# Twelve-bit gated projection: halves of the output product behind the first and second block of the next quarter, value halves added up in PSUM

## The chip, the core and the metric

The kernel runs on one core of a Trainium2 chip. The core has a matrix engine (PE, with a separate lane PEld for the weight loads), a vector engine (DVE), a scalar engine (ACT), a general engine (POOL) and a queue that issues transfers (SP). Each takes its instructions in the order of its own queue; an instruction starts when the results it needs are there. PE writes into PSUM, which has eight banks of 128 x 512 numbers here; DVE and ACT read and write PSUM and SBUF, POOL only SBUF. The metric is the device time of one execution in microseconds (us); the median of three runs before is 2509.24 us (2509.1 to 2509.75).

## The reference

The inputs are 1024 rows of 512 numbers, a graph, and 16 blocks of conditions. A graph layer is followed by four equal layers of cross attention and a gated feed-forward part, and a second graph layer. The change touches the feed-forward part alone:

```python
for i in range(L):                              # L = 4
    a = _attn(_ln(h, ...), cond, Wq[i], Wk[i], Wv[i], Wo[i])
    h = h + a
    u = _ln(h, ln3_w[i], ln3_b[i]) @ geglu_w[i] + geglu_b[i]    # 512 -> 4096
    val, gate = jnp.split(u, 2, axis=-1)
    f = val * jax.nn.gelu(gate, approximate=False)              # 1024 x 2048
    h = h + f @ ffo_w[i] + ffo_b[i]                             # 2048 -> 512
```

## The kernel before

All large products are made by a scheme that needs seven block products where eight are usual (two by two blocks; the sums of blocks that it needs are made by POOL and DVE). The 2048 columns of the feed-forward part are taken in four **quarters** r of 512, and each quarter in four **blocks** c of 128 columns. One block yields `f` for its 128 columns and all 1024 rows: two tiles of 128 x 512, here f0 and f1 (`a11`/`a12` and `a21`/`a22` of the output product). When the four blocks of a quarter are there, `ffn_out` (L1309) multiplies them with the quarter's output weights and adds to `h`. It does so in two **halves** s = 0, 1, each seven products of eight PE instructions. In a half the products run in the order 0, 6, 4, 5, 1, 3, 2. Products 0 and 6 read only tiles of blocks 0 and 1. Products 4, 5 and 2 read the sums `fs` (s1, s2, s4), which need blocks 2 and 3. Products 1 and 3 add to the banks of 0 and 6, so they wait until DVE has read those: `kept` (L1329) and `hall` (L1325).

Quarter 0 is made with plain 32-bit products (class `Quad`, with the banks ga, gb, gc, gd). Beside it ACT and DVE split the normalised rows into high and low parts (`begin_right` L1084 makes gr, `finish_right` L1093 makes gl), because quarters 1 to 3 are made with "twelve-bit" products: both factors split into a high part and a low part, three matmuls for one (class `Chunk`, L1113). A Chunk's weights are loaded by four transfers (`__init__`, tiles gxa and gxb), summed by POOL (`sums`, L1139, the last sum into gy), and split by `split` (L1101: ACT makes the high part gha or ghb, DVE the low part gla or glb, POOL the third factor gsa or gsb); the part with the suffix a serves products 0, 5, 6, 4, the part with b products 1 and 3. Product 2 stays a 32-bit product, made from gy (L1215). In the tables all banks of a Chunk are called g.

`Chunk.steps` (L1184) is a generator: between its yields the main loop (L1801) runs parts of the block before. Before, one turn of the loop for block n gives PE this order: the first parts of products 0 and 5 of n; then, of block n-1, product 2 into bank `d` (L1215, behind the DVE addition `add(g1, d, u3)` of L1209, shown as L1190, that has to read d first) and the end of product 1; the end of 0 and the first part of 6; the end of 3 of n-1; the end of 5; then the first parts of 4, 1 and 3 with the ends of 6 and 4 between. DVE has in a turn, in this order: the value v1 (L1218) and f1 = v1 x g1 (L1220) of n-1, the addition for u2 of n, f0 of n-1 (L1226), the sums of f of n-1 (`sums_of_f`, L1289: one subtraction for blocks 0 and 1, which POOL makes, L1294; three for blocks 2 and 3, on DVE, L1296 to L1298), u3, glb of n+1, the two additions onto scaled banks (L1173) with g1 between them, and gla of n+2 (L1104).

The order of nearly all of this is fixed: `pin` (L1099) puts an instruction behind the one traced before it on its engine. Instructions without `pin` are ordered by the scheduler of the language: the earliest in the program among those whose inputs it takes to be there, so that work from further down fills a wait. `ffn_out` is pinned for quarters 1 and 2, and not for quarters 0 and 3. For quarters 1 and 2 both halves stand behind the turn of block 0 of the next quarter (L1827).

Buffers: 36 slots of 128 x 1024 (`slots`), ten tiles of 128 x 512 (`work`, t512), six accumulators (`accs`), and two single tiles with the tags row and last (`rows`).

## Time and profile before

| | |
|---|---|
| median of the runs | 2509.24 us |
| time of the profiled execution | 2509.91 us |
| its span, first to last instruction | 2508.1 us |
| mean granted PE clock | 0.99 |
| ACT busy | 840.8 us (34%) |
| POOL busy | 1052.3 us (42%) |

The profile is of one execution. A row of waits names who waited, for which instruction, the sum, how often, and the longest. A row of the timeline has the start, the duration, engine, line, operation and tiles, and in brackets the idle time ahead of it and what ended that. A row by stage has, behind the bounds and the length, the busy time of PE, PEld, DVE, ACT and POOL with instruction counts, then the granted PE clock as a share of full speed, and the share of the transfer engines. A group row has count, busy time, mean duration in ns, and idle time ahead.

### The profile page before, as it was taken

Reading aid. Unit: us, or ns where it says so; the run is one execution under the profiler, and the core shown is the slowest. Engines: PE = TensorE matmul, PEld = TensorE weight load, DVE = VectorE, ACT = ScalarE, POOL = GpSimd, SP = SyncE. Lnnn points to the kernel's source line nnn. Section 1 sums busy time; section 2 is a strip of 40 time slices with the busy share of each in tenths; the row PEclk is TensorE's granted clock in tenths of the full one; section 3 lists DMA queues with packets and bytes.
Section 4 is the critical chain, followed back from the end, with each engine's and each line's share of the span. In section 5 each row is a group of like instructions: output and inputs, shape, how many; then the busy total and the mean of one; then the engine's idle time right before and its main releaser. Section 6 shows DMA issues by size and latency. Waiting matters only on the chain. (4 is left out here: it accounts for less than half of the span.)

```text
span 2508.1 us, 35093 instructions
## 1 busy us (share of the span) xinstructions
PE 2418.3 (96%) x13032; PEld 1887.7 (75%) x13032; DVE 1740.1 (69%) x3224; ACT 840.8 (34%) x1784; POOL 1052.3 (42%) x1083
## 2 busy tenths in 40 slices
PE   8999999998999999999999999999999999999999
PEld 5778886676787887567787888477777888567677
DVE  9666567877676557786686556786795556787764
ACT  7323334333223334342313334432223333432320
POOL 0433444366553223274563224254474322435641
PEclk9999999999999999999999999999999999999999
DMA  5422220111312210011222121011132031011140
GB/s 176 130 74 97 97 85 22 47 50 35 113 39 76 93 64 22 19 58 47 64 92 72 72 76 35 13 55 43 42 130 68 14 122 51 5 47 51 34 143 35
DMA packets 118066, 163.56 MB, mean 65 GB/s; under 512 B 9256, under 2 KB 66928, under 8 KB 117888
## 3 DMA queue, kind: packets, MB, share of 16 engines
q1 hardware_dynamic: 115792, 155.81, 19.1%
q0 software_dynamic: 1376, 4.30, 0.5%
q8 instruction: 107, 1.75, 0.3%
q10 hardware_dynamic: 720, 1.11, 0.1%
q14 instruction: 71, 0.58, 0.1%
HBM read 138.12 MB, written 23.07 MB: 64 GB/s over the span
## 5 line engine op out<-in xcount | busy, mean ns | idle before, releaser
L1105 POOL TENSOR_TENSOR gsa<-gha,gla 128x1024 fp32r<-128x1024 f32 x48 | 115.9, 2415 | 175.3 <-DVE gla L1104 170.5
L1169 ACT ACTIVATE g<-g 128x512 f32<-128x512 f32 x192 | 108.0, 574 | 238.1 <-PE g L1155 236.5
L799 ACT ACTIVATE pr<-sc,nmax 128x256 f32<-128x256 f32 x256 | 118.2, 471 | 91.9 <-DVE nmax L794 91.4
L1182 ACT ACTIVATE g<-g,gcols 128x512 f32<-128x512 f32 x96 | 67.5, 703 | 223.6 <-DVE g L1190 214.3
L300 PE MATMUL fa<-wff,fT 128*128 128x256 f32 x512 | 125.6, 386 | 14.2 <-DVE kept L1329 14.2
L1215 PE MATMUL g<-ln3T,gy 128*128 128x512 f32 x192 | 103.3, 665 | 37.2 <-DVE g L1190 37.2
L997 POOL TENSOR_TENSOR kr<-ct,ct 128x256 f32<-128x256 f32 x48 | 36.9, 768 | 211.8 <-DVE pr L804 207.2
L300 PEld LDWEIGHTS fa<-wff,fT 128*128 128x128 f32 x512 | 98.0, 193 | 34.6 <-DVE kept L1329 17.4
L300 PE MATMUL pa_v<-wv,ct 128*128 128x256 f32 x512 | 124.0, 385 | 0.0
L1155 PE MATMUL g<-gr,gsa 128*128 128x512 f32 x384 | 121.4, 398 | 0.9
L1155 PE MATMUL g<-gr,gha 128*128 128x512 f32 x384 | 122.0, 399 | 0.0
L1294 POOL TENSOR_TENSOR fT<-fT,fT 128x512 f32<-128x512 f32 x24 | 30.9, 1288 | 217.1 <-DVE fT L1226 217.1
L300 PE MATMUL pc_v<-wv,ct 128*128 128x256 f32 x512 | 121.0, 379 | 0.0
L300 PE MATMUL pd_v<-wvs,ct 128*128 128x256 f32 x512 | 121.0, 379 | 0.0
L1155 PE MATMUL g<-gl,gla 128*128 128x512 f32 x384 | 119.0, 391 | 0.0
L794 DVE TENSOR_REDUCE nmax<-sc 128x2 f32<-128x512 f32 x128 | 83.7, 678 | 41.2 <-PE sc L787 41.2
L1104 DVE SCALAR_TENSOR_TENSOR gla<-gha,gxa 128x1024 fp32r<-128x1024 f32 x48 | 76.5, 1594 | 51.3 <-ACT gha L1103 51.3
L300 PEld LDWEIGHTS pa_v<-wv,ct 128*128 128x128 f32 x512 | 94.9, 190 | 22.5 <-issue 9.2
L300 PEld LDWEIGHTS pd_v<-wvs,ct 128*128 128x128 f32 x512 | 97.3, 190 | 13.2
L300 PEld LDWEIGHTS pc_v<-wv,ct 128*128 128x128 f32 x512 | 97.0, 190 | 13.0
L1215 PEld LDWEIGHTS g<-ln3T,gy 128*128 128x128 f32 x192 | 37.4, 205 | 75.3 <-DVE g L1190 46.9
L804 DVE TENSOR_SCALAR pr<-pr,inv 128x256 f32<-128x256 f32 x256 | 90.4, 395 | 2.9
(518 smaller groups left out, 6474.5 us busy)
## 6 DMA issues: line engine op xcount, KB each, us to landing
ct<-cond_dram SPq DMA_DIRECT2D x72, 512.0 KB, 5.3
wff<-in_L_gnn_ffo_w_dram SPq DMA_DIRECT2D x32, 512.0 KB, 4.1
cond_dram<-ct SPq DMA_DIRECT2D x24, 512.0 KB, 3.0
gxa<-in_L_gnn_geglu_w_dram SPq DMA_DIRECT2D x96, 128.0 KB, 2.2
gxb<-in_L_gnn_geglu_w_dram SPq DMA_DIRECT2D x96, 128.0 KB, 2.2
cond<-in_L_gnn_cond_dram SPq DMA_DIRECT2D x32, 256.0 KB, 4.7
ct<-cond_dram SPq DMA_DIRECT2D x24, 256.0 KB, 5.6
wk<-in_L_gnn_Wk_dram SPq DMA_DIRECT2D x8, 512.0 KB, 4.3
```

The source lines that it names most:

```text
L300: each(nc.tensor.matmul(at, left[:, k, l0:l1], right[:, k, r0:r1], start=start and n == 0 and k == 0, stop=n == len(cols_of) - 1 and k == ...
L794: nc.vector.tensor_reduce(nmax, ps3, AX.X, OP.max, negate=True)
L799: nc.scalar.activation(pr3[:, a, :], ps3[:, a, :], AF.Exp, bias=nmax[:, a:a + 1], accum_out=tot[:, a:a + 1])
L804: scores.last = nc.vector.tensor_scalar(pr3[:, a, :], pr3[:, a, :], inv[:, a:a + 1], None, OP.mult)
L997: t.tensor_tensor(to, of, less, OP.subtract)
L1104: pin(nc.vector.scalar_tensor_tensor(l.bitcast(F32R), h, -1.0 / TINY, x, OP.mult, OP.add))
L1105: pin(nc.gpsimd.tensor_tensor(s.bitcast(F32R), h, l, OP.subtract))
L1155: pin(nc.tensor.matmul(to, self.part(i, which)[:, k, :], self.rights[i][which].bitcast(F32R)[:, k, :], start=start and k == 0, stop=stop a ...
L1169: pin(nc.scalar.mul(to, to, 1.0 + TINY))
L1182: pin(nc.scalar.activation(to, of, AF.Gelu, bias=gcols[:, cg:cg + 1]))
L1215: pin(nc.tensor.matmul(d, self.last[:, k, :], self.rights[2][:, k, :], start=False, stop=k == 1, skip_group_check=True))
L1294: each(t.tensor_tensor(a21, a11, a21, OP.subtract))
```

## The change

It has these parts:

- Within a turn the end of product 1 of block n-1 comes first, and product 2 of n-1 (into `d`) comes behind the end of product 3, so behind 22 instead of 12 twelve-bit PE instructions after the end of product 4.
- v1 and f1 are replaced: DVE adds u2 to d in PSUM (`add(d, d, u2)`), and f1 = (d + bias) x g1 is read from PSUM. f0 comes before them.
- All sums of f are made by DVE; they stand behind the turn, after the split of the low part, which itself moves from between u3 and the scaled banks to the end of the turn.
- The split of the next weights' high part and the load (`split_next`) move from the end of the turn for n+2 to the place behind the first two products, for n+1 (in the turns of blocks 1 to 3 of quarter 1 and block 3 of later ones, and of block 0 of quarters 2 and 3); for blocks 0 and 1 of quarters 2 and 3 one such split stands ahead of a half.
- The two halves of `ffn_out` of quarters 1 and 2 stand behind blocks 0 and 1 of the next quarter, one each. `ffn_out` of quarter 0 is pinned. The load of the next output weights follows the second half.
- The low parts gl for products 0 and 1 are made during quarter 0's third block, 5 and 6 ahead of the first half, 4 and 3 between the halves.
- `add_bias` runs for all eight row blocks at once ahead of quarter 0's end, where the last two were added at the layer's end.
- Buffers: `kept` is two t512 instead of a slot, gy takes the single tiles row and last, the tiles of f are taken block by block, and v1's accumulator is gone.

```diff
--- before.py
+++ after.py
...
@@ -1113,14 +1113,13 @@
     class Chunk:
 
 
...
         def __init__(self, l, r, c):
             self.n, self.c = f"{l}_{r}_{c}", c
             self.cv = l * 2 * DFF // P + r * KC + c
             self.x = [flat(slot(f"gxa_{self.n}")), t512(f"gxb_{self.n}")]
             if c % 2 == 0:
-                Chunk.room = t512(f"gy_{self.n}")
+                tag = ("row", "last")[c // 2]
+                Chunk.room = rows.tile([P, D], F32, tag=tag, name=f"gy_{self.n}")
             self.last = columns_of(Chunk.room)[:, c % 2]
             for k, n in enumerate((2, 1)):
                 for j in range(2):
@@ -1181,7 +1180,7 @@
             cg = self.cv + DFF // P
             pin(nc.scalar.activation(to, of, AF.Gelu, bias=gcols[:, cg:cg + 1]))
 
-        def steps(self, aside):
+        def steps(self, sum_next, split_low):
 
 
             n, bias = self.n, gcols[:, self.cv:self.cv + 1]
@@ -1199,31 +1198,29 @@
             yield
             add(u2, self.end(5), s1)
             yield
-            aside[0]()
+            sum_next()
             self.scale(4)
             add(u3, self.end(6), u2)
-            aside[1]()
             self.scale_onto(1, s1)
             g1 = acc_tile(f"g1_{n}")
             d = self.end(4)
             add(g1, d, u3)
             self.gate(g1, g1)
             self.scale_onto(3, u3)
-            aside[2]()
+            split_low()
             yield
-            for k in range(2):
-                pin(nc.tensor.matmul(d, self.last[:, k, :], self.rights[2][:, k, :], start=False,
-                                     stop=k == 1, skip_group_check=True))
-            v1 = acc_tile(f"gv1_{n}")
-            pin(nc.vector.scalar_tensor_tensor(v1, d, bias, u2, OP.add, OP.add))
-            f0, f1 = (self.fT[i][self.c // 2][:, self.c % 2, :] for i in range(2))
-            pin(nc.vector.tensor_tensor(f1, v1, g1, OP.mult))
             a = self.end(1)
             yield
             g0 = acc_tile(f"g0_{n}")
             self.gate(g0, self.end(3))
+            for k in range(2):
+                pin(nc.tensor.matmul(d, self.last[:, k, :], self.rights[2][:, k, :], start=False,
+                                     stop=k == 1, skip_group_check=True))
+            f0, f1 = self.f.of(self.c)
+            pin(nc.vector.scalar_tensor_tensor(f0, a, bias, g0, OP.add, OP.mult))
+            add(d, d, u2)
             yield
-            pin(nc.vector.scalar_tensor_tensor(f0, a, bias, g0, OP.add, OP.mult))
+            pin(nc.vector.scalar_tensor_tensor(f1, d, bias, g1, OP.add, OP.mult))
 
     class KeyPair(InStep):
 
@@ -1279,47 +1276,61 @@
         return {i: inner_right(nc.gpsimd, *(x[i][:, k, :] for k in range(2) for x in of), quarters(room))
                 for i, room in zip(INNER[0] + INNER[1], rooms)}
 
-    def f_slots(l, r):
-        return ([slots_of(2, f"fT_{l}_{r}_{i}") for i in range(2)], slots_of(3, f"fs_{l}_{r}"))
-
...
-    def sums_of_f(fT, s, c, t=nc.vector, each=lambda ins: ins):
-        k = c % 2
-        a11, a12, a21, a22 = (fT[i][j][:, k, :] for i in range(2) for j in range(2))
-        s1, s2, s4 = (x[:, k, :] for x in s)
-        if c < 2:
-            each(t.tensor_tensor(a21, a11, a21, OP.subtract))
-        else:
+    class Gated:
+
+
+        def __init__(self, l, r):
+            self.n, self.tiles, self.s = f"{l}_{r}", [], None
+
+        def of(self, c):
+            if c == len(self.tiles):
+                self.tiles.append(slot(f"fT_{self.n}_{c}"))
+            return [self.tiles[c][:, i, :] for i in range(2)]
+
+        def sums(self, c, t=nc.vector, each=lambda ins: ins):
+            if c < 2:
+                a11, a21 = self.of(c)
+                each(t.tensor_tensor(a21, a11, a21, OP.subtract))
+                return
+            if c == 2:
+                self.s = slots_of(3, f"fs_{self.n}")
+            (a11, a21), (a12, a22) = self.of(c - 2), self.of(c)
+            s1, s2, s4 = (x[:, c % 2, :] for x in self.s)
             each(t.tensor_tensor(s2, a22, a21, OP.subtract))
             each(t.tensor_tensor(s1, s2, a11, OP.add))
-            sums_of_f.last = each(t.tensor_tensor(s4, a12, s2, OP.subtract))
+            Gated.last = each(t.tensor_tensor(s4, a12, s2, OP.subtract))
+
+        def left(self):
+            blocks = [[self.of(2 * j + k)[i] for k in range(2)] for i in range(2) for j in range(2)]
+            return order7(blocks, *([x[:, k, :] for k in range(2)] for x in self.s))
+
...
     def ffn_out(l, r, s, left, right, kept, each=lambda ins: ins):
...
         n = f"{l}_{r}_{s}"
-        u = kept[:, s, :]
+        u = kept[s]
         a, b, c, d = (bank(f"{x}_{n}") for x in ("fa", "fb", "fc", "fd"))
         h11, h12, h21, h22 = (hall[:, 4 * i + 2 * s:4 * i + 2 * s + 2, j * M:(j + 1) * M]
                               for i in range(2) for j in range(2))
 
         def product(i, to, start):
-            multiply(to, left[i], right[i],
-                     [((2 * s + q) * P, (2 * s + q + 1) * P, 0, M) for q in range(2)], start,
-                     each)
+            for q in range(2):
+                for k in range(2):
+                    each(nc.tensor.matmul(to[:, q * M:(q + 1) * M],
+                                          left[i][k][:, (2 * s + q) * P:(2 * s + q + 1) * P],
+                                          right[i][:, k, :], start=start and q == 0 and k == 0,
+                                          stop=q == 1 and k == 1, skip_group_check=True))
 
         def add(to, of):
             each(nc.vector.tensor_tensor(to, halves_of(of), to, OP.add))
...
     def load_projections(l):
...
-        wv_summed = weight_sums.last
         next_cond(l, 0)
         wq, wo, ffb = load_rest(l)
-        with waiting_for(sums_of_f.last, mybir.EngineType.Pool):
-            with tc.issue_after(wv_summed.ins):
-                for nb in range(NB - 2, NB):
-                    summed = add_bias(nb)
-            with tc.issue_after(summed.ins):
-                wq = weight_sums(wq, f"wqs_{l}")
+        with waiting_for(Gated.last, mybir.EngineType.Pool):
+            wq = weight_sums(wq, f"wqs_{l}")
         return wk, wv, (wq, weight_sums.spare), wo, ffb, spare
 
     def load_last():
...
@@ -1736,7 +1742,7 @@
         ln3_turn(g, (1, 1))
         summed = ln3_sums(nc.vector, g)
         with tc.issue_after(summed.ins):
-            for nb in range(NB - 2):
+            for nb in range(NB):
                 add_bias(nb)
         quads[2].second()
         quads[3].second()
@@ -1744,20 +1750,27 @@
 
         last = l == L - 1
         lnT = None
-        kept = slot(f"kept_{l}")
+        kept = [t512(f"kept_{l}_{i}") for i in range(2)]
         raw_out = load_out(l, 0)
         more = [slot(f"gr_{l}_{i}") for i in range(2 * len(SPLIT) - 2)]
         wide = four_wide(f"gr_{l}")
         more.extend(wide[:, 2 * i:2 * i + 2, :] for i in range(2))
         begun = {i: (right[i], *more[2 * n:2 * n + 2]) for n, i in enumerate(SPLIT)}
+        Chunk.rights = {2: right[2]}
+
+        def finish_rights(*of):
+            for i in of:
+                Chunk.rights[i] = finish_right(f"gl_{l}_{i}", *begun[i])
 
         def parts_beside(c):
             with tc.issue_after(quads[c].last.ins):
                 for i in SPLIT[2 * c:2 * c + 2]:
                     begin_right(f"gt_{l}_{i}", *begun[i])
+                if c == 2:
+                    finish_rights(0, 1)
 
         wff = out_weights(nc.gpsimd, l, 0, raw_out)
-        geglu(quads, fT, fS, parts_beside)
+        geglu(quads, f, parts_beside)
         chunks = [(r, c) for r in range(1, R) for c in range(KC)]
         ready = []
 
@@ -1765,88 +1778,69 @@
             if chunks:
                 ready.append(Chunk(l, *chunks.pop(0)))
 
-        def prepare(n, *what):
+        def sum_chunk(n):
             if n < len(ready):
-                for do in what:
-                    if do is None:
-                        ready[n].sums()
-                    else:
-                        ready[n].split(do)
+                ready[n].sums()
+
+        def split(n, low):
+            if n < len(ready):
+                ready[n].split(low)
 
         load()
-        prepare(0, None)
-
-        def finish_rights(*of):
-            for i in of:
-                Chunk.rights[i] = finish_right(f"gl_{l}_{i}", *begun[i])
-
-        Chunk.rights = {2: right[2]}
-        finish_rights(0, 5)
-        ffn_out(l, 0, 0, left_of_f(fT, fS), wff, kept)
-        prepare(0, False, True)
-        finish_rights(6, 4)
+        sum_chunk(0)
+        finish_rights(5, 6)
+        ffn_out(l, 0, 0, f.left(), wff, kept, pin)
+        split(0, False)
+        split(0, True)
         load()
-        prepare(1, None)
-        ffn_out(l, 0, 1, left_of_f(fT, fS), wff, kept)
-        finish_rights(1, 3)
-        prepare(1, False)
+        sum_chunk(1)
+        finish_rights(4, 3)
+        ffn_out(l, 0, 1, f.left(), wff, kept, pin)
+        split(1, False)
         load()
         raw_out = load_out(l, 1)
 
-        def finish_chunk(flow, c):
-            next(flow, None)
-            sums_of_f(fT, fS, c, *((nc.gpsimd, pin) if c < 2 else (nc.vector, pin)))
+        def split_next(n):
+            split(n, False)
+            load()
 
         before = None
         for r in range(1, R):
             for c in range(KC):
                 chunk = ready.pop(0)
-
-                def sum_next():
-                    prepare(1, None)
-
-                def split_low():
-                    prepare(0, True)
-
-                def split_next():
-                    prepare(1, False)
-                    load()
-
-                flow = chunk.steps([sum_next, split_low, split_next])
+                flow = chunk.steps(lambda: sum_chunk(1), lambda: split(0, True))
+                chunk.f = f if c else Gated(l, r)
                 next(flow)
+                if c > 2 or r == 1 and c or r > 1 and c == 0:
+                    split_next(0)
+                for _ in range(3):
+                    if before:
+                        next(before, None)
+                    next(flow)
                 if before:
-                    next(before)
-                next(flow)
-                if before:
-                    next(before)
-                next(flow)
-                if before:
-                    finish_chunk(before, (c - 1) % KC)
-                next(flow)
+                    f.sums((c - 1) % KC, nc.vector, pin)
                 before = flow
                 if c == 0:
-                    if r > 1:
-                        for s in range(2):
-                            ffn_out(l, r - 1, s, left_of_f(fT, fS), wff, kept, pin)
+                    kept_f, f = f, chunk.f
+                if r > 1 and c < 2:
+                    split_next(1)
+                    ffn_out(l, r - 1, c, kept_f.left(), wff, kept, pin)
+                    if c == 1:
                         raw_out = load_out(l, r)
-                    fT, fS = f_slots(l, r)
-                elif c == (KC - 1 if r + 1 < R else KC - 2):
+                if c == (KC - 1 if r + 1 < R else KC - 2):
                     wff = out_weights(nc.gpsimd, l, r, raw_out)
-                chunk.fT = fT
-        for _ in range(2):
-            next(before)
-        finish_chunk(before, KC - 1)
-        fT = left_of_f(fT, fS)
+        for _ in range(3):
+            next(before, None)
+        f.sums(KC - 1, nc.vector, pin)
+        fT = f.left()
         if last:
             w_out, base, again, dinv_row = load_last()
-            with waiting_for(sums_of_f.last, mybir.EngineType.Pool):
-                for nb in range(NB - 2, NB):
-                    add_bias(nb)
+            with waiting_for(Gated.last, mybir.EngineType.Pool):
                 w_out = out_weights(nc.gpsimd, L, 0, w_out)
             ffn_out(l, R - 1, 0, fT, wff, kept)
         else:
             lnT = [slots_of(2, f"ln2T_{l + 1}_{i}") for i in range(2)]
-            projections = load_projections(l + 1, add_bias)
+            projections = load_projections(l + 1)
             ffn_out(l, R - 1, 0, fT, wff, kept)
             ready_first(l + 1, [0, 1, 4, 5])
             ffn_out(l, R - 1, 1, fT, wff, kept)
```

23 lines of the change are left out of this document (10 added, 13 removed).

## The prediction

> **What bounds the kernel now.** I read the page first. PE is the bound: it is busy nearly all of the span, so what can be won is PE's waiting.
>
> ```profile
> PE 2418.3 (96%) x13032; PEld 1887.7 (75%) x13032; DVE 1740.1 (69%) x3224; ACT 840.8 (34%) x1784; POOL 1052.3 (42%) x1083
> ```
>
> Then the waits of the weight loads, which show better than the modelled matmuls where PE stands still:
>
> ```profile
> PEld g L1215 <- DVE g L1190: 46.9, 23, 3.5
> ...
> PEld fa L300 <- DVE kept L1329: 17.4, 8, 3.7
> ...
> PEld fc L300 <- DVE hall L1325: 11.9, 4, 3.0
> ```
>
> All three are waits on DVE in the feed-forward part: product 2 waits for g1, a half for `kept`, quarter 0's second half for `hall`. The timeline of weight loads gives the pace: product 2 of the first and of the last block of each layer, and between them, in layer 0, one wait and two products of a half.
>
> ```profile
> 497.59 0.41 PEld L1215 LDWEIGHTS g<-ln3T,gy 128*128 128x128 f32 x2
> ...
> 532.67 0.50 PEld L1215 LDWEIGHTS g<-ln3T,gy 128*128 128x128 f32 x2 [3.52 <-DVE g L1190]
> ...
> 545.36 1.70 PEld L300 LDWEIGHTS fc<-wff,fT 128*128 128x128 f32 x8
> 547.09 1.70 PEld L300 LDWEIGHTS fd<-wffs,fs 128*128 128x128 f32 x8
> ...
> 677.80 0.30 PEld L1215 LDWEIGHTS g<-ln3T,gy 128*128 128x128 f32 x2 [1.90 <-DVE g L1190]
> ...
> 1081.44 0.41 PEld L1215 LDWEIGHTS g<-ln3T,gy 128*128 128x128 f32 x2
> ...
> 1260.85 0.30 PEld L1215 LDWEIGHTS g<-ln3T,gy 128*128 128x128 f32 x2 [1.86 <-DVE g L1190]
> ...
> 1664.50 0.41 PEld L1215 LDWEIGHTS g<-ln3T,gy 128*128 128x128 f32 x2
> ...
> 1844.68 0.30 PEld L1215 LDWEIGHTS g<-ln3T,gy 128*128 128x128 f32 x2 [1.87 <-DVE g L1190]
> ...
> 2248.34 0.41 PEld L1215 LDWEIGHTS g<-ln3T,gy 128*128 128x128 f32 x2
> ...
> 2424.86 0.41 PEld L1215 LDWEIGHTS g<-ln3T,gy 128*128 128x128 f32 x2
> ```
>
> And three stages of layer 0, each beginning where product 2 of a block begins:
>
> ```profile
> core 0: us, PE busy (x) PEld busy (x) DVE busy (x) ACT busy (x) POOL busy (x), PEclk, DMA share, GB/s
> 497.59:507.58 9.99, 9.99 (x41) 7.51 (x40) 9.04 (x10) 4.73 (x9) 6.79 (x6) 1.00 0.13 37
> 518.98:532.67 13.69, 10.49 (x40) 7.36 (x40) 12.21 (x14) 5.62 (x10) 10.40 (x10) 0.97 0.16 44
> 532.67:543.60 10.93, 10.92 (x31) 7.42 (x32) 7.02 (x8) 5.49 (x9) 7.87 (x6) 0.72 0.00 0
> ```
>
> From one product 2 to the next is one turn. The first stage is a turn of 9.99 in which PE never stands, the second one of 13.69 with the wait of 3.52. Where DVE has 9.04 of work PE does not wait; where it has 12.21, PE does. Behind the long wait the granted clock is 0.72 for 10.93, some 3 lost: a long wait is paid twice.
>
> A half is seven products at 547.09 - 545.36 = 1.73, so 12.1. Undisturbed, the eleven turns and four halves between a layer's first and last row take 11 x 9.99 + 4 x 12.1 = 158.3. They took 180.2, 179.4, 180.2 and 176.5: 21.9 + 21.1 + 21.9 + 18.2 = **83.1 us** too long. That is what can be won in quarters 1 to 3.
>
> **DVE's durations**, group means of layer 0's stretch from 480 to 705, with ACT's high part:
>
> ```profile
> L1220 DVE TENSOR_TENSOR fT<-gv,g 128x512 f32<-128x512 f32 x12 | 21.5, 1792 | 0.6
> L1104 DVE SCALAR_TENSOR_TENSOR gla<-gha,gxa 128x1024 fp32r<-128x1024 f32 x11 | 18.4, 1672 | 13.0 <-ACT gha L1103 13.0
> L1104 DVE SCALAR_TENSOR_TENSOR glb<-ghb,gxb 128x512 fp32r<-128x512 f32 x11 | 12.3, 1116 | 0.0
> ...
> L1218 DVE SCALAR_TENSOR_TENSOR gv<-g,gcols,gu 128x512 f32<-128x512 f32 x12 | 8.9, 744 | 9.0 <-PE g L1215 9.0
> ...
> L1226 DVE SCALAR_TENSOR_TENSOR fT<-g,gcols,g 128x512 f32<-128x512 f32 x12 | 8.9, 738 | 0.0
> L1297 DVE TENSOR_TENSOR fs<-fs,fT 128x512 f32<-128x512 f32 x6 | 8.3, 1392 | 0.2
> L1173 DVE SCALAR_TENSOR_TENSOR g<-g,gs 128x512 f32<-128x512 f32 x12 | 8.2, 685 | 0.0
> ...
> L1298 DVE TENSOR_TENSOR fs<-fT,fs 128x512 f32<-128x512 f32 x6 | 7.3, 1212 | 0.0
> L1296 DVE TENSOR_TENSOR fs<-fT,fT 128x512 f32<-128x512 f32 x6 | 6.1, 1013 | 0.0
> ```
> ```profile
> L1103 ACT ACTIVATE gha<-gxa 128x1024 fp32r<-128x1024 f32 x11 | 11.6, 1051 | 19.1 <-POOL gxa L1139 18.9
> ```
>
> Single rows of the timeline: f1 twice and a short gla on DVE, then POOL's two products of a split.
>
> ```profile
> 523.63 2.33 DVE L1220 TENSOR_TENSOR fT<-gv,g 128x512 f32<-128x512 f32 x1
> ...
> 534.36 1.23 DVE L1104 SCALAR_TENSOR_TENSOR gla<-gha,gxa 128x1024 fp32r<-128x1024 f32 x1 [1.13 <-ACT gha L1103]
> ...
> 647.76 0.69 DVE L1220 TENSOR_TENSOR fT<-gv,g 128x512 f32<-128x512 f32 x1
> ```
> ```profile
> 520.59 1.27 POOL L1105 TENSOR_TENSOR gsb<-ghb,glb 128x512 fp32r<-128x512 f32 x1
> 523.02 2.40 POOL L1105 TENSOR_TENSOR gsa<-gha,gla 128x1024 fp32r<-128x1024 f32 x1 [1.16 <-DVE gla L1104]
> ```
>
> f1 takes 0.69 alone and 2.33 while POOL makes gsa. Instructions that read a bank (L1173, L1218, L1226) keep to 0.69 to 0.74 in the mean, those on two SBUF tiles (f1, gla, glb, the sums) do not.
>
> **The change part by part.**
>
> *Value in PSUM.* v1 and f1 (0.744 + 1.792) become an addition into a bank (taken as L1173, 0.685, which also writes one; no row shows the very form) and an f1 with the form of f0 (0.738): 1.1 less on DVE a turn. A turn's eight instructions on banks are 6 x 0.685 + 2 x 0.738 = 5.6; with gla and glb (2.8) that is 8.4.
>
> *Sums of f.* Blocks 0 and 1: one subtraction comes from POOL to DVE, 0.69 free to 1.39 held: 9.1 to 9.8 a turn, under 9.99. Blocks 2 and 3: three, 1.0 + 1.4 + 1.2 = 3.6 held, 2.1 free: 10.5 to 12.0, over 9.99. Both of these now fall into the turn of block 0 of the next quarter. With the half behind it PE has 22.1 there, DVE 8.4 + 3.6 + 3.6 + 1.7 (a second gla) + 6 x 0.685 = 21.4.
>
> *Product 2 later, the end of product 1 earlier.* Product 2 is reached ten twelve-bit instructions later; a turn of 9.99 has 36 of them and product 2, which I put at one 1.73, so 8.26 / 36 = 0.23 each, 2.3 together. But the end of product 1 now stands where product 2 stood and waits for its scaled bank, which DVE makes one instruction (0.69) before g1. So the move alone wins only 0.69 of each wait; DVE's lighter turn has to win the rest. In the turns with 9.1 to 9.8 it does.
>
> *Split later.* Behind the first two products (8 x 0.23 = 1.8) come the high part (1.05), gla (1.7) and gsa (2.4): gsa ends some 7 into a turn and is needed behind ten instructions of the next, at 9.99 + 2.3 = 12.3. Some 5 are spare, and I cost it at nothing. Loads and POOL's weight sums move with it in SP's and POOL's queues; POOL loses the subtraction on which it stood waiting.
>
> *A half behind block 0, one behind block 1.* The second has DVE nearly free: no cost. In the first, product 4 needs s1 of block 3. Since the last turn's end DVE then has glb, three sums, gla, eight on banks, glb and two sums: 1.1 + 3.6 + 1.7 + 5.6 + 1.1 + 2.4 = 15.5 held, 0.7 + 2.1 + 1.2 + 5.6 + 0.7 + 1.4 = 11.7 free. PE gets there after 9.99 + 2 x 1.73 - 0.7 = 12.7. The wait is 0 to 2.8, with the clock's 3 up to 5.8. POOL has output weights to sum there, so I take 2.4, near the held end: two a layer, **+19** (0 to 46).
>
> *Quarter 0, pinned.* Its weight loads and one DVE row:
>
> ```profile
> 457.69 0.19 PEld L300 LDWEIGHTS fa<-wff,fT 128*128 128x128 f32 x1 [0.24 <-issue]
> ...
> 459.20 0.41 PEld L300 LDWEIGHTS gc<-ln3S,wgate 128*128 128x128 f32 x2
> ...
> 485.00 1.59 PEld L300 LDWEIGHTS fc<-wffs,fT 128*128 128x128 f32 x8 [2.97 <-DVE hall L1325]
> ...
> 488.35 0.41 PEld L1155 LDWEIGHTS g<-gr,gha 128*128 128x128 f32 x2
> ```
> ```profile
> 469.67 0.68 DVE L1297 TENSOR_TENSOR fs<-fs,fT 128x512 f32<-128x512 f32 x1
> ```
>
> Before, a half's product (fa) filled in ahead of block 3's own (gc) while DVE was late. Pinned, it cannot: products 0 and 6 follow block 3, product 4 waits for s1 (469.67 + 0.68 = 470.35), and from there twelve products remain, 20.8. Quarter 1 begins at 491.1 instead of 488.35: +2.8, the 2.97 being gone. The low parts for products 0 and 1 (1.2 each, as gla) now stand ahead of block 3's work on DVE, s1 up to 2.4 later; or one low part and an addition leave its way, 1.9 earlier. So 0.9 to 5.2, with the clock to 8.2; I take 3.5, close to the first figure: four layers, **+14** (4 to 33).
>
> *Layer's end.* Three sums (3.6) now stand ahead of block 3's f0, product 2 behind it is ready sooner. **+4** (-5 to +6, a sum or so a layer either way). `add_bias` and the buffers: the waits of PE above name neither, so nothing.
>
> **Sum**: 2509.9 - 83.1 + 19 + 14 + 4 = 2463.8 against the profiled execution's own 2509.91, which is 0.7 above the median; so **2463**. Low ends: -83.1 + 0 + 4 - 5 = -84, 2425. High ends: -83.1 + 46 + 33 + 6 = +2, 2511.
>
> **Rivals.**
>
> *The wait only moves* to the end of product 1. If DVE stays as late, each wait of product 2 loses 0.69: 23 x 0.69 = 16, less quarter 0's 14: 2507. For it: the row of 3.52. Against it: f1's 1.79 and block 2's three sums leave the tight turn.
>
> *The split comes too late* (slower): PE stands in each turn for gsa. Some seven turns a layer take it this way, 28; the gain of 46 is used up when gsa is 46 / 28 = 1.6 beyond the spare 5, and at 3 beyond it the time is 2463 + 84 = 2547. For it: high part, gla and gsa are in series within a turn, and gla is held by 0.4 in the mean (1.67 against 1.23). Against it: the 5.
>
> *The moved subtractions are held by gsa*: 24 turns of 8.4 + 0.69 + 2.40 = 11.5, 1.5 over: +36, 2499. For it: f1's 2.33. Against it: the subtraction stands in the queue ahead of the gla for which gsa waits, so only gsb (1.27) meets it. The Trainium skill's page "SBUF — State Buffer", section "SBUF: two separate sides", has the port that DVE and POOL share as an exclusive lock, which a DVE instruction with two SBUF inputs takes for its whole length; by that rule this case is possible. The two rows of f1 agree with it.
>
> *Nothing is left of the waits*: sums free, quarter 0 even: 2509 - 83 = 2426. For it: the free durations above; against it: POOL is busy where they fall.
>
> **How the numbers follow.** Forecast 0.58, wait only moves 0.11, split too late 0.13, subtractions held 0.05, nothing left 0.13. A measurement of this kernel tells about 0.2% (5 us) from no change. Faster: 0.58 + 0.13 + 0.05 + half of 0.11, 0.82; same 0.05; slower 0.13. The range 2430 to 2499 leaves out the slower cases, most of the moved wait and the lowest tail, 2 in 10; the forecast's own is 2445 to 2485.
>
> **What would show it.** Right: product 2's wait on g1 gone, turns of 9.99, f1 at 0.74, a wait of the first half's product 4 on s1 (2 to 3 us, quarters 1 and 2), quarter 1 beginning 2 to 5 later. Wrong: the end of product 1 waiting on a scaled bank, the end of product 0 waiting on gsa, or PE waiting long inside quarter 0.

## The result, and the profile after

The changed kernel takes 2485.7 us in the median, against 2509.5 for the kernel before in the same session: a ratio of 0.9905 (0.9888 to 0.9922). It is faster by 24 us where 46 were forecast; 2485.7 lies inside the range of 2430 to 2499 and just above the forecast's own 2445 to 2485. The profiled execution has a span of 2486.1 against 2508.1. The page's busy times, then the waits of the weight loads:

```profile
PE 2407.7 (97%) x13032; PEld 1888.3 (76%) x13032; DVE 1696.2 (68%) x3248; ACT 839.6 (34%) x1784; POOL 1012.4 (41%) x1059
```
```profile
PEld fd L1330 <- DVE fs L1300: 40.1, 15, 4.0
...
PEld gd L300 <- DVE g L970: 22.5, 8, 5.8
```

The three waits of before are gone or nearly so: on g1 (46.9, now none), on `kept` (17.4, now 1.0) and on `hall` (11.9, now 1.5). Two others stand in their place: product 4 of a half waits for s1, and in quarter 0 the last block's product waits for DVE. The timeline of layer 0's weight loads, with product 2 in L1217 and the halves in L1330:

```profile
526.85 0.42 PEld L1217 LDWEIGHTS g<-ln3T,gy 128*128 128x128 f32 x2
...
536.80 0.42 PEld L1217 LDWEIGHTS g<-ln3T,gy 128*128 128x128 f32 x2
...
546.11 0.41 PEld L1330 LDWEIGHTS fd<-wffs,fs 128*128 128x128 f32 x2
550.49 2.20 PEld L1330 LDWEIGHTS fd<-wffs,fs 128*128 128x128 f32 x6 [3.97 <-DVE fs L1300]
552.79 2.08 PEld L1330 LDWEIGHTS fb<-wffs,fs 128*128 128x128 f32 x8
...
564.19 0.42 PEld L1217 LDWEIGHTS g<-ln3T,gy 128*128 128x128 f32 x2
...
586.26 0.42 PEld L1217 LDWEIGHTS g<-ln3T,gy 128*128 128x128 f32 x2
```

A plain turn is 9.95 (526.85 to 536.80), in every layer. The turn with the second half is 22.07. The turn with the first half is 27.39, 5.3 too long: 3.97 of wait, and 1.35 because the loads behind it run slowly (2.20 for six and 2.08 for eight, where eight take 1.70). The eight turns of this kind are together 43.1 too long.

By stage, from the first load of one to the first load of the next (quarter 0 from its first load into the bank gb, behind earlier loads into ga that fill in among the work before it):

| us, layers 0 to 3 | before | after | sum |
|---|---|---|---|
| quarter 0 | 61.47, 63.15, 63.15, 63.15 | 67.85, 67.32, 66.74, 67.09 | +18.1 |
| quarters 1 to 3 and the layer's last product | 215.09, 214.30, 215.09, 210.76 | 204.79, 205.00, 201.47, 203.18 | -40.8 |
| between the layers, each | 305.6 | 305.6 | 0 |

The second row is the 83.1 of waits, less 43.1 in first halves, and 0.8 of other things. With +0.7 ahead of layer 0 the rows give the 22.0 between the two spans.

### The profile page after: what moved, and what is told of

The parts are those of the page before. It is cut to its first block, busy times and chain, and to the rows that moved or that the text cites. A ratio compares the mean times of both kernels' runs of the same rounds, so it can differ in the third digit from the quotient of the medians.

```text
span 2486.1 us, 35090 instructions
## 1 busy us (share of the span) xinstructions
PE 2407.7 (97%) x13032; PEld 1888.3 (76%) x13032; DVE 1696.2 (68%) x3248; ACT 839.6 (34%) x1784; POOL 1012.4 (41%) x1059
## 5 line engine op out<-in xcount | busy, mean ns | idle before, releaser
L1168 ACT ACTIVATE g<-g 128x512 f32<-128x512 f32 x192 | 112.1, 584 | 311.5 <-PE g L1154 307.7
L1105 POOL TENSOR_TENSOR gsb<-ghb,glb 128x512 fp32r<-128x512 f32 x48 | 79.9, 1664 | 215.4 <-DVE glb L1104 215.4
L1154 PE MATMUL g<-gr,gsa 128*128 128x512 f32 x384 | 136.6, 437 | 0.0
L1330 PE MATMUL fa<-wff,fT 128*128 128x256 f32 x512 | 124.4, 385 | 0.2
L1330 PEld LDWEIGHTS fa<-wff,fT 128*128 128x128 f32 x512 | 99.6, 195 | 21.3 <-issue 5.0
L1330 PE MATMUL fd<-wffs,fs 128*128 128x256 f32 x256 | 71.9, 418 | 34.1 <-DVE fs L1300 34.1
L1154 PEld LDWEIGHTS g<-gr,gsa 128*128 128x128 f32 x384 | 71.9, 188 | 33.4 <-issue 16.3
L1220 DVE SCALAR_TENSOR_TENSOR fT<-g,gcols,g 128x512 f32<-128x512 f32 x48 | 35.9, 749 | 80.1 <-ACT g L1181 79.8
```

Source lines behind the costliest of these rows:

```text
L1105: pin(nc.gpsimd.tensor_tensor(s.bitcast(F32R), h, l, OP.subtract))
L1154: pin(nc.tensor.matmul(to, self.part(i, which)[:, k, :], self.rights[i][which].bitcast(F32R)[:, k, :], start=start and k == 0, stop=stop a ...
L1168: pin(nc.scalar.mul(to, to, 1.0 + TINY))
L1220: pin(nc.vector.scalar_tensor_tensor(f0, a, bias, g0, OP.add, OP.mult))
L1330: each(nc.tensor.matmul(to[:, q * M:(q + 1) * M], left[i][k][:, (2 * s + q) * P:(2 * s + q + 1) * P], right[i][:, k, :], start=start and q ...
```

## The experiments

Every kernel but the last is the changed kernel with one part altered, or two (e9, e10). Its worth is its ratio less 0.9905, times 2509 (+ is slower); with intervals of some 0.0017 on each side that is good to about 6 us.

| run | altered | median, us | ratio to the kernel before | worth, us |
|---|---|---|---|---|
| e1 | block 3's sums ahead of the next block's chain | 2509.6 | 1.0000 (0.9991 to 1.0010) | +24 |
| e2 | both halves behind block 1 | 2504.3 | 0.9977 (0.9967 to 0.9987) | +18 |
| e3 | quarter 0 not pinned | 2470.8 | 0.9842 (0.9826 to 0.9859) | -16 |
| e4 | quarter 0's low parts at their old places | 2471.3 | 0.9849 (0.9832 to 0.9865) | -14 |
| e5 | value in SBUF | 2496.8 | 0.9951 (0.9935 to 0.9968) | +12 |
| e6 | both halves behind block 0 | 2495.4 | 0.9946 (0.9930 to 0.9963) | +10 |
| e7 | product 2 at its old place | 2504.8 | 0.9982 (0.9973 to 0.9992) | +19 |
| e8 | POOL's output weights one block earlier | 2470.7 | 0.9848 (0.9832 to 0.9865) | -14 |
| e9 | value and product 2 as before | 2515.5 | 1.0015 (1.0005 to 1.0024) | +28 |
| e10 | split and POOL's subtraction as before | 2540.6 | 1.0119 (1.0102 to 1.0136) | +54 |
| e12 | only the split as before | 2540.2 | 1.0112 (1.0089 to 1.0135) | +52 |
| e11 | three repairs together | 2429.5 | 0.9674 (0.9658 to 0.9690) | -58 |

### The first half's wait: e1 and e2

My first theory was the order on DVE: s1 stands behind some 6 us of the next block's work. e1 puts the three sums ahead of that work, in that turn alone:

```diff
-                for _ in range(3):
+                early = r > 1 and c == 0
+                for i in range(3):
                     if before:
                         next(before, None)
+                    if early and i == 2:
+                        f.sums(KC - 1, nc.vector, pin)
                     next(flow)
-                if before:
+                if before and not early:
                     f.sums((c - 1) % KC, nc.vector, pin)
```

> Only in the turn of block 0 of quarters 2 and 3, the three sums of block 3 stand right behind its f1 on DVE, ahead of the new block's chain (u3, the end of product 4, g1) and of glb. Theory 'order on DVE': s1 of the first half comes late because some 6 us of the new block's work stand ahead of it; s1 is then ready within 0.5 of PE's arrival, the waits on s1 (3.6 to 4.0 each) go, the eight turns of a first half (six of them above 27) come down to 22.0 to 22.5, and the time falls by 8 x 5 = 40, to about 2445. Rival 'amount of work on DVE and POOL': sums beside gsa and the weight sums are stretched, the half's own additions come late in their turn, and a wait of the half on kept or on a scaled bank takes the place of the one on s1; then no more than 10 is won, 2475 or more.

It became slower than the changed kernel. The waits of e1's weight loads:

```profile
PEld fa L1330 <- DVE kept L1340: 41.3, 8, 5.4
...
PEld fd L1330 <- DVE fs L1300: 19.1, 15, 2.1
```

s1 is earlier, but the half's own addition to `kept` is pinned behind everything else on DVE, and product 1 waits for it, 5.1 to 5.4 each. The theory of order fell. The rival held: with either order something of DVE's comes late in this turn, s1 or the addition to `kept`.

e2 puts both halves behind block 1:

```diff
-                    ffn_out(l, r - 1, c, kept_f.left(), wff, kept, pin)
+                    if c == 1:
+                        for s in range(2):
+                            ffn_out(l, r - 1, s, kept_f.left(), wff, kept, pin)
```

> Both halves of a quarter's output product stand behind block 1 of the next quarter. Theory 'order on DVE': s1 has been ready for a turn, no half waits; but two turns in a row (of block 3 and of block 0) now carry three sums each with 9.99 of PE's time, 10.5 to 12.0 of work on DVE, so one to three us of wait arise in the turns of blocks 0 and 1: the time falls by 15 to 43, 2443 to 2471. Rival 'amount of work': DVE cannot catch up without a half behind block 0, waits of 3 and more on scaled banks with half clock behind them, 2486 or more.

No half of quarters 1 and 2 waits for s1 any more, but the turn of block 0 takes 16.83, with one wait of 5.03 in it, which ends at 550.60. The profile puts it down to POOL's gy, which had ended at 550.04; ACT's rows show what PE needs next:

```profile
548.95 1.06 ACT L1103 ACTIVATE gha<-gxa 128x1024 fp32r<-128x1024 f32 x1 [1.86 <-POOL gxa L1138]
549.91 1.06 ACT L1168 ACTIVATE g<-g 128x512 f32<-128x512 f32 x2
```

The scaling of the next products (L1168) stands on ACT behind the high part gha, which waits for POOL's weight sums, and these stand behind the four sums of the output weights (536.95 to 543.96) and gsa. So POOL is late first. (That PE waited for the scaling is read from these times; the profile does not name it.)

### POOL's output weights: e8

```diff
-                if c == (KC - 1 if r + 1 < R else KC - 2):
+                if c == KC - 2:
                     wff = out_weights(nc.gpsimd, l, r, raw_out)
```

> POOL's four sums of the output weights (6.9 in all, between gsb and gsa in the turn of block 0) are put one block earlier in quarters 1 and 2, all else as changed. Theory 'POOL's weight sums make the backlog': beside them two of block 2's sums take 1.67 and 1.75, gla 2.31, against 0.7 to 1.2 free, and gsa comes late; without them s1 of block 3 is ready 2 to 3 earlier, its wait falls from 3.97 to about 1 and the clock stays up: each first half turn loses 3 to 5, 2486 - (24 to 40) = 2446 to 2462, less what the turn of block 3 now waits. Rival 'DVE's work alone': the sums meet gsa or gsb instead, s1 comes no more than 0.5 earlier, and the turn of block 3, where POOL now has 14 of work in 9.95, waits for gsa: 2486 to 2510.

The first halves come down to 23.75 and 23.26 in layer 0. Most of the sums of f and gla are shorter (gla 1.21 for 2.31), and POOL's output weights no longer stand beside them. But it gains 14 only: in quarter 1 the turn of block 3 takes 13.87. There the scheduler set the output weights ahead of POOL's weight sums for the next block. gha then waited 3.36 for those sums, gla 3.19 for gha, and PE 1.09 and 2.11. Both theories held a part: the weights make the backlog, and a badly chosen new place makes another.

### Quarter 0: e3 and e4

e3 leaves the two halves of quarter 0 to the scheduler, e4 puts the low parts back:

```diff
-        ffn_out(l, 0, 0, f.left(), wff, kept, pin)
+        ffn_out(l, 0, 0, f.left(), wff, kept)
...
-        ffn_out(l, 0, 1, f.left(), wff, kept, pin)
+        ffn_out(l, 0, 1, f.left(), wff, kept)
```
```diff
-                if c == 2:
-                    finish_rights(0, 1)
...
-        finish_rights(5, 6)
+        finish_rights(0, 5)
         ffn_out(l, 0, 0, f.left(), wff, kept, pin)
...
+        finish_rights(6, 4)
...
-        finish_rights(4, 3)
         ffn_out(l, 0, 1, f.left(), wff, kept, pin)
+        finish_rights(1, 3)
```

> Quarter 0's two halves are left to the scheduler again, the low parts stay in the new order. Quarter 0 (from its first product to the first twelve-bit product) took 61.5, 63.15, 63.15, 63.15 in the kernel before and 67.9, 67.3, 66.7, 67.1 in the changed one, 18 more in all. Theory 'pin': the half's products fill PE's wait for g1 of block 3 again, quarter 0 comes back to 62 to 64 in each layer, 2467 to 2472. Rival 'low parts': g1 and s1 are late because low parts 0 and 1 stand ahead on DVE; whatever fills the wait, the end of the half comes as late, 2482 to 2486.

> Quarter 0's halves stay pinned, the low parts of the weights go back to their old places (0 and 5 behind block 3, 6 and 4 behind the first half's product, 1 and 3 behind the second). Theory 'pin' (2.8 of the 3.5 forecast for a layer): quarter 0 stays above 66, 2482 to 2486. Rival 'low parts' (two of 1.2 to 2.4 each ahead of g1 on DVE): quarter 0 comes down by 2 to 5 a layer, 2466 to 2478; the wait for hall ahead of the second half (3.0 before) may come back then.

In e3 quarter 0 takes 62.46, 62.04, 62.02, 62.12; in e4 64.96, 63.27, 63.26, 63.27. Against the changed kernel's sum e3 is 20 less and e4 14 less, so either one brings back most or all of the 18, and the cost lay in neither alone. The two low parts ahead of block 3's g1 on DVE make PE wait for it, 5.25 in layer 1; the pin keeps the half's products from filling that wait. With the wait shorter (e4: 2.99) three layers take 0.1 more than in the kernel before, and layer 0 3.5 more; with the pin off (e3) the low parts cost nothing (2.3 less than before in all). For e4 I had expected the pin to carry most, which was wrong.

### The parts of the change, undone: e5, e6, e7, e9, e10, e12

Which part took the 83 away? e5 puts the value back into an SBUF tile, e7 product 2 back ahead of the end of product 1, e6 both halves behind block 0, e9 the whole end of a block. The edit of e5:

```diff
-            add(d, d, u2)
+            v1 = acc_tile(f"gv1_{n}")
+            pin(nc.vector.scalar_tensor_tensor(v1, d, bias, u2, OP.add, OP.add))
             yield
-            pin(nc.vector.scalar_tensor_tensor(f1, d, bias, g1, OP.add, OP.mult))
+            pin(nc.vector.tensor_tensor(f1, v1, g1, OP.mult))
```

> The value half of a block goes through an SBUF tile again (v1 written by DVE from the bank, f1 from two SBUF tiles), product 2 and everything else stays where the change put it. Theory 'DVE's lighter turn': f1 goes back from 0.75 to 1.2 to 2.3, each turn of DVE grows by some 1; the plain turns (9.1 to 9.8 on DVE, 9.95 on PE) reach their limit and the turns with three sums go beyond it: 24 turns with up to 1 more, and the wait on s1 1 longer: 2495 to 2515. Rival 'product 2's place': the waits went because product 2 comes later on PE, DVE has time enough: 2484 to 2492.

> Product 2 of a block stands ahead of the end of product 1 again, 10 matmuls (2.3) earlier on PE; DVE's order, the value in PSUM and all else stay changed. Theory 'DVE's lighter turn': in a plain turn of the changed kernel g1 is added at 533.0 and product 2 would now be reached at 534.5, so plain turns stay at 9.95, and only the turns with three sums wait 0 to 1 each: 2484 to 2496. Rival 'product 2's place' (the move is what took the waits away): waits on g1 come back in most turns, 1 to 3 each with the clock behind them: 2510 or more.

> Both halves stand behind block 0 of the next quarter, as in the kernel before; all else as changed. Theory after the last runs ('backlog of DVE and POOL in the turn of block 0'): what is late at the first half's product 4 is late all the same, and behind the second half DVE has caught up: 2483 to 2490, with the first half's wait on s1 and no other. Rival 'the parting of the halves carries the gain': the kernel before waited 17.4 for kept in its halves and up to 3.5 for g1 in the turn behind them; such waits come back, 2500 or more.

> The whole end of a block is as it was: product 2 ahead of the end of product 1, v1 in SBUF and f1 from it ahead of f0 on DVE. Halves, split, sums of f and quarter 0 stay changed. Each of the two parts alone cost 10 (value in SBUF) and 18 (product 2) and left the plain turns at 9.95 to 10.0. Theory 'the block's end as a whole took the waits': product 2 waits for g1, v1 for product 2, and the chain of DVE behind it makes the next g1 late; with both undone plain turns rise to 10.5 or more, waits on g1 come back, 2510 to 2540. Rival 'POOL's part did it' (split later, subtraction to DVE): the two costs add at most, plain turns at 10.0 or below, 2490 to 2512.

e5 keeps plain turns at 9.95; it only makes the wait on s1 longer (45.0 in all). It lies in the range of the theory of a lighter DVE, but for one of its two reasons alone. e7 keeps plain turns at 9.99, as that theory has it, but costs 19 instead of up to 10: the waits on s1 reach 5.1. In e6 the first half loses the same 5.5, and the waits on `kept` stay away (1.0), so the parting of the halves did not take them. The time lies between the two ranges given, for the turn of block 1 behind the halves takes 10.79: there the high part again stands on ACT ahead of the scaling, and PE waits 0.97. e9 lies in the range of its first theory, but waits on g1 come back in quarter 1 alone (turns of 10.35 and 10.97, 6.2 us in all four layers), not the 46.9. Its worth is 28, some 20 of it in first halves.

e12 moves only the split of the weights back: that of part b (ghb, glb, gsb, in the code the low one) behind u3, that of part a (gha, gla, gsa, the high one) to the end of a turn. e10 also gives POOL the subtraction of blocks 0 and 1. The middle of e12's edit:

```diff
             add(u3, self.end(6), u2)
+            split_low()
             self.scale_onto(1, s1)
...
             self.scale_onto(3, u3)
-            split_low()
+            split_high()
...
```

> The split of the weights stands at its old places in a turn (low part b right behind u3, high part a at the turn's end) and the subtraction of blocks 0 and 1 is POOL's again; the block's end, the halves and quarter 0 stay changed. Theory 'POOL's part did it': POOL stands waiting for f1 with the weights' sums behind it, the high part, gla and gsa come late, plain turns rise above 10.5: 2500 to 2530. Rival 'the block's end did it': plain turns stay at 9.95, 2480 to 2494.

> Only the split of the weights stands at its old places in a turn; the subtraction of blocks 0 and 1 stays on DVE, all else as changed. In the run with both undone, plain turns took 10.66 to 10.71, PE standing 0.84 to 0.88 at the end of product 0, for which ACT had the scaling behind the high part of the split. Theory 'the split's place in ACT's queue': plain turns of quarters 1 and 2 take 10.6 to 10.7 here too, and most of the 55 comes back: 2515 to 2540. Rival 'POOL's subtraction': plain turns fall to 9.95 to 10.2 and the time to 2485 to 2505.

Both are slower than the kernel before, and alike, so with the split at its old places the subtraction's place is worth nothing. In quarters 1 and 2 of e12 a plain turn takes 10.64 to 10.67; the first halves take 31.96 and 31.87 in layer 0, with 7.2 of wait on s1. Of the 52 some 14 lie in plain turns (five a layer by 0.7) and 36 in first halves (eight by 4.5). Which of the two splits carries this was not tried. One turn's end in ACT's queue, first e12's and then the changed kernel's:

```profile
534.65 0.73 ACT L1181 ACTIVATE g<-g,gcols 128x512 f32<-128x512 f32 x1 [2.02 <-DVE g L1189]
535.29 1.04 ACT L1103 ACTIVATE gha<-gxa 128x1024 fp32r<-128x1024 f32 x1
536.24 1.05 ACT L1168 ACTIVATE g<-g 128x512 f32<-128x512 f32 x2
```
```profile
523.18 0.72 ACT L1181 ACTIVATE g<-g,gcols 128x512 f32<-128x512 f32 x1 [2.16 <-DVE g L1189]
523.80 0.62 ACT L1103 ACTIVATE ghb<-gxb 128x512 fp32r<-128x512 f32 x1
524.33 1.25 ACT L1168 ACTIVATE g<-g 128x512 f32<-128x512 f32 x2
525.49 1.05 ACT L1103 ACTIVATE gha<-gxa 128x1024 fp32r<-128x1024 f32 x1
```

In e12 the first scaling (L1168) stands behind gha, and the next product of PE waits 0.85, until about the time at which the first of these two scalings is done. The row names nothing that ended the wait, so that it is the scaling is read from the times:

```profile
536.92 0.30 PEld L1154 LDWEIGHTS g<-gr,gsa 128*128 128x128 f32 x2 [0.85 <-issue]
```

In its first half s1 comes late since gla, with a wait, stands ahead of block 3's sums, and the sum for s1 takes 2.71 beside POOL's gsa, against 1.10 in the changed kernel:

```profile
550.18 1.99 DVE L1104 SCALAR_TENSOR_TENSOR gla<-gha,gxa 128x1024 fp32r<-128x1024 f32 x1 [1.40 <-ACT gha L1103]
...
552.80 2.71 DVE L1301 TENSOR_TENSOR fs<-fs,fT 128x512 f32<-128x512 f32 x1
```

Is this what made PE wait for g1 in the kernel before? There the same place of a turn, and DVE's gla in two turns:

```profile
518.96 0.72 ACT L1182 ACTIVATE g<-g,gcols 128x512 f32<-128x512 f32 x1 [4.22 <-DVE g L1190]
519.85 1.06 ACT L1103 ACTIVATE gha<-gxa 128x1024 fp32r<-128x1024 f32 x1 [0.17 <-POOL gxa L1139]
```
```profile
509.51 2.02 DVE L1104 SCALAR_TENSOR_TENSOR gla<-gha,gxa 128x1024 fp32r<-128x1024 f32 x1 [1.42 <-ACT gha L1103]
...
520.94 2.00 DVE L1104 SCALAR_TENSOR_TENSOR gla<-gha,gxa 128x1024 fp32r<-128x1024 f32 x1 [1.41 <-ACT gha L1103]
```

Behind one more addition, gla is the next thing on DVE. It waits for gha, gha for the activation of g1 (L1182) and here 0.17 more for POOL, and the activation for DVE's g1, which ends a turn. This is a closed loop through two engines, and DVE stands still in it once a turn. Two long turns, the first in the row below and the second in the prediction, are just DVE's work and this wait: 9.94 + 1.42 = 11.36 of 11.40, and 12.21 + 1.41 = 13.62 of 13.69.

```profile
507.58:518.98 11.40, 10.57 (x43) 7.44 (x41) 9.94 (x11) 5.64 (x10) 8.19 (x8) 1.00 0.31 85
```

The split's new place did not cut this loop. Below are the groups of gla and glb in the changed kernel, and of gla in e12:

```profile
L1104 DVE SCALAR_TENSOR_TENSOR gla<-gha,gxa 128x1024 fp32r<-128x1024 f32 x12 | 19.5, 1625 | 4.0 <-ACT gha L1103 4.0
...
L1104 DVE SCALAR_TENSOR_TENSOR glb<-ghb,gxb 128x512 fp32r<-128x512 f32 x12 | 9.3, 774 | 6.6 <-ACT ghb L1103 6.6
```
```profile
L1104 DVE SCALAR_TENSOR_TENSOR gla<-gha,gxa 128x1024 fp32r<-128x1024 f32 x12 | 16.2, 1350 | 12.3 <-ACT gha L1103 12.3
```

DVE's wait for gha was 13.0 a layer before, is 4.0 after, and 12.3 again with the split back. But for ghb, on which it did not wait before, it now waits 6.6, so 10.6 in all. And in e12 and e10, where the wait for gha is back, no product 2 waits for g1. What fell is DVE's own work. Two plain turns of the changed kernel, then the two turns of e9 in which PE waits for g1 (DVE's work is the third of the engines' figures):

```profile
506.96:516.90 9.94, 9.94 (x41) 7.51 (x40) 7.79 (x12) 5.41 (x10) 6.81 (x6) 1.00 0.18 53
516.90:526.85 9.95, 9.95 (x42) 7.52 (x40) 7.98 (x12) 5.42 (x10) 6.95 (x7) 1.00 0.20 55
```
```profile
513.50:523.85 10.35, 10.35 (x42) 7.51 (x40) 8.98 (x11) 4.94 (x9) 7.32 (x6) 1.00 0.21 61
523.85:534.82 10.97, 10.23 (x41) 7.44 (x40) 9.53 (x12) 5.41 (x9) 7.30 (x6) 1.00 0.24 66
```

In the changed kernel DVE waits 0.57 + 0.83 = 1.40 for ACT's high parts in each of these two turns, as much as before; with 7.98 of work this stays below PE's 9.95. In e9 it waits 1.35 and 1.41, and 8.98 + 1.35 = 10.33 of 10.35 and 9.53 + 1.41 = 10.94 of 10.97 fill the turn again. e7 has product 2 as early as e9, but 7.9 to 8.0 of work in these turns, and no wait on g1; what e9 adds is v1 and an f1 that stands earlier and takes 2.3 beside gsa. So in these turns the waits on g1 went because DVE's work fell, and not because of the split or of product 2's place. (In e5 the value in SBUF makes DVE's turn no heavier, 7.8 and 7.9: f1 stands behind f0 there and takes 0.86 in the mean.)

e9 keeps one part of this: the place of block 2's three sums. Before, they stood ahead of g1 in the turn of 13.69, with 3.1 of its 12.21:

```profile
527.15 0.79 DVE L1296 TENSOR_TENSOR fs<-fT,fT 128x512 f32<-128x512 f32 x1
527.97 1.11 DVE L1297 TENSOR_TENSOR fs<-fs,fT 128x512 f32<-128x512 f32 x1
529.00 1.22 DVE L1298 TENSOR_TENSOR fs<-fT,fs 128x512 f32<-128x512 f32 x1
```

Now they stand behind that g1 and reach into the long turn of block 0. The eight turns of this kind had 3.5 of wait each, 28 of the 46.9. That moving the sums took most of that is worked out from these rows; no run put them back, and none tells what took the waits on `kept`.

### Three repairs: e11

POOL's output weights are pinned behind the weight sums of block 2's turn, block 3's sums stand ahead of glb, and quarter 0 is not pinned:

```diff
...
+                def sum_beside():
+                    sum_chunk(1)
+                    if c == KC - 2:
+                        summed.append(out_weights(PinnedPool, l, r, raw_out))
+
+                def split_beside():
+                    if r > 1 and c == 0:
+                        f.sums(KC - 1, nc.vector, pin)
+                    split(0, True)
...
```

> Three edits together on the changed kernel: POOL's sums of the output weights are pinned behind the weight sums of block 2's turn in each of quarters 1 to 3 (not between gsb and gsa of block 0's turn); block 3's three sums stand ahead of glb in the turn of block 0; quarter 0's halves are not pinned. Theory 'backlog of POOL and DVE in the turn of block 0, and the pin in quarter 0': the eight turns of a first half, 5.4 too long each, come to 22.1 to 22.6, a gain of 36 to 43; quarter 0 gives 19, as alone: 2485.7 - 19 - 40 = 2427, range 2424 to 2436; no wait in the turn of block 3 (13.87 in the run with the weights one block earlier), since the weights' sums no longer stand ahead of those of the next block. Rival 'the wait only moves': gsb or gsa behind the weights' sums comes late in block 3's turn, 2 to 4 in each of the eight: 2443 to 2465.

2429.5 is within the range given: 82 less than the kernel before in its session, and by the ratios 58 less than the changed kernel. (PinnedPool passes each of POOL's sums through `pin`.) Quarter 2's first half in layer 0, with no wait left in it, then layer 0's quarters 1 to 3 as one stage:

```profile
595.82 0.42 PEld L1223 LDWEIGHTS g<-ln3T,gy 128*128 128x128 f32 x2
...
605.13 1.70 PEld L1336 LDWEIGHTS fd<-wffs,fs 128*128 128x128 f32 x8
606.86 1.70 PEld L1336 LDWEIGHTS fb<-wffs,fs 128*128 128x128 f32 x8
...
617.89 0.42 PEld L1223 LDWEIGHTS g<-ln3T,gy 128*128 128x128 f32 x2
```
```profile
489.15:683.44 194.29, 193.15 (x818) 153.63 (x817) 146.74 (x212) 64.20 (x105) 114.34 (x98) 1.00 0.24 74
```

That turn is 22.07, like the second half's. PE is busy 193.15 of 194.29, where the changed kernel took 204.79 for the same work. How the gain parts between the weights' place and that of the sums was not tried. Against what was expected, the turn of block 3 in quarter 1 takes 10.38 and quarter 1's first half 22.89 in layer 0, with 0.94 on s1, and quarter 0 still waits 2.1 for `hall` in each layer.

## Why the prediction came out as it did

- **The 83.1 of waits.** The size was right: plain turns are 9.95, second halves 22.07, and nearly all that is too long now lies in first halves. The reason for the waits on g1, a lighter turn of DVE, agrees with the rows: its work is 7.8 and 8.0 in plain turns, where I had put 9.1 to 9.8, f1 takes 0.74 as forecast, and where the work is heavier again the waits come back (e9). The move of product 2, for which I had counted 0.69 of each wait, is not needed for that: without it no product 2 waits for g1 (e7), and only with the value's form and place undone as well do 6.2 return. The rest of the g1 waits, by the rows, went with block 2's three sums, which I had named; no run tested that alone.
- **The split, at nothing.** I looked at its new place only for a loss and found 5 spare. Its old place would have cost the changed kernel 52 (e12), in ACT's queue and in first halves, so the forecast rests on a part that I had not seen the need of, and that it came out near is partly luck. These worths add to more than the whole gain: they are taken from the changed kernel one at a time, and do not say how much of the 83.1 each part won.
- **The first half, +19.** The mechanism was right: product 4 waits for s1. The size was not. A turn lost 5.4 instead of 2.4, together 43 instead of 19. That is the main miss: 24, as much as the whole of what the spans differ by from the forecast (22.0 gained, 46.1 forecast); the other terms cancel. It lies near the held end of the bounds, 46. DVE reached s1 at 3.97 past PE's arrival, with 0.57 and 0.76 of waiting for ACT's ghb that my sum did not have, and gla at 2.31 instead of 1.7. Behind such a wait the clock fell, which I had in the bounds and left out of the value.
- **Quarter 0, +14.** It came to +18.1. The sum was close, its make-up was not, so its closeness is luck: I gave 2.8 of 3.5 a layer to the pin, but the pin alone costs 3.8 in all four layers (e4), the low parts alone nothing (e3). Together they cost 3.6 to 6.4 a layer, and PE's wait of 5.3 to 5.8 inside quarter 0 is one that I had named as a sign of being wrong.
- **Layer's end, +4.** With the remaining terms it is -0.8, inside the bounds.
- **The rivals.** "The wait only moves" and "the split comes too late" did not come: no product waits for gsa, and the later split was needed (e12). "Subtractions held by gsa" fell: in the changed kernel they take 0.685 in the mean, and giving them back to POOL changed nothing (e10 against e12). "Nothing left of the waits" is what e11 reached in these quarters, by moving POOL's sums of the output weights and those of block 3.

## What to carry to other kernels

Where an engine is late, add up its busy time and its own idle time within one turn: if the two make up the turn, that engine sets the pace, also where another one shows the wait. Then follow the idle time back, since it can close a loop through a second engine; but moving an instruction in that engine's queue may only move the wait (here from gha to ghb), while taking work off the late engine or out of its tight turn shortened the turn. Undoing one part at a time does not share out a gain when the parts hide or uncover each other's waits. Before pinning a group of instructions, see what it was filling. When a wait moves from one tile to the next as the order changes (s1, `kept`, the scaling), the stage may have too much work, and then some has to leave it, as POOL's weight sums did in e11.

## What the runs showed of the hardware

*DVE and POOL.* In this case a DVE instruction on two SBUF tiles does not merely slow down beside POOL, it seems to wait. In e12 POOL's gsa started first (537.67 for 2.75), and the sum that DVE began at 538.23 ended with it:

```profile
538.23 2.74 DVE L1301 TENSOR_TENSOR fs<-fs,fT 128x512 f32<-128x512 f32 x1
```

It ended at 540.97, 0.55 behind gsa's end at 540.42; the same sum took 0.68 in the kernel before (469.67, in the prediction). The Trainium skill's page "SBUF — State Buffer", section "SBUF: two separate sides", has the port as an exclusive lock that whichever starts first holds for its whole length; the 2.74 agrees.

*The clock.* The same wait of 2.97 for `hall` was followed in layer 0 of the kernel before by eight loads in 1.59 (its row stands in the prediction), and in layer 1 by eight in 2.48:

```profile
1067.17 2.48 PEld L300 LDWEIGHTS fc<-wffs,fT 128*128 128x128 f32 x8 [2.97 <-DVE hall L1325]
```

Two stages, in the changed kernel behind the wait of 3.97 and in e8 behind waits of 1.09 and 2.11 that lie 7.3 apart (the granted clock is the third number from the end):

```profile
550.40:552.70 2.30, 2.21 (x5) 1.83 (x6) 2.30 (x3) 0.00 (x0) 1.16 (x1) 0.50 0.00 0
```
```profile
540.60:543.00 2.40, 2.40 (x5) 1.19 (x4) 2.40 (x4) 1.16 (x2) 0.44 (x1) 0.59 0.00 0
```

The clock was 0.50 and 0.59, though neither wait in e8 is long alone. In the changed kernel the eight waits for s1 are all 3.97 or 3.98, and the turns with them take 26.28 to 28.68. So the length of one wait does not tell its second price. The Trainium skill's page "TensorE: Matmul & The Clock Gate", section "Part 1: The HAM clock gate (the "warmup" mystery)", has the activity watched in a free-running window, by which one wait can be paid once or twice; the two rows with 2.97 agree.
